# A selective-scan layer inside a two-layer transformer kernel: C's rows in SBUF and the scan's items in pairs

## The chip, the cores and the metric

The kernel is one program on one core of a Trainium2 chip. Its time is the device time of one execution in microseconds (us), as the median of several. In the profile PE is the tensor engine (PEld its weight loads), DVE the vector engine, ACT the scalar engine, POOL GpSimd and SP the engine from whose queue nearly all DMAs are issued.

## The reference

The input is x, 8 rows of 512 time steps and 256 channels. Two layers are added to it, each a conditioned attention part and a conditioned expert part:

```python
x = x + attn0(cond0(x))     # attn0: a selective state-space layer (below)
x = x + ffn0(cond2_0(x))    # 8 experts, top 2, gelu MLP
x = x + attn1(cond1(x))     # 8 heads of softmax attention over 512 steps
x = x + ffn1(cond2_1(x))    # 32 experts, top 4, swiglu, and a shared swiglu
```

cond0 ends in a normalization of its own; cond2_1 is a small adapter with a layer norm behind it. The part that the change is about is attn0, with 512 inner channels and 16 states:

```python
xc, z = split(x @ W_in.T); xc = silu(conv4(xc))
dt, B, C = split(xc @ W_x.T, [64, 80])
delta = softplus(dt @ W_dt.T + b_dt); A = -exp(A_raw)
# over time, for every inner channel d and state n:
h[n, d] = exp(delta[d] * A[n, d]) * h[n, d] + delta[d] * B[n] * xc[d]
y[d] = sum_n C[n] * h[n, d] + D[d] * xc[d]
out = (y * silu(z)) @ W_out.T
```

## The kernel before

Time lies along the free axis (T = 512), channels along the 128 partitions; a row of 256 channels is a tile [128, 2, 512], all in fp32. Two Python generators emit the work. thread_x does attn0 for the eight rows and stores each finished row to DRAM (xa). thread_y does ffn0 and attn1 for groups of rows ([0], [1, 2], [3, 4, 5], [6, 7]). The main loop at the end draws from both in turn by the numbers that they yield (XROW, YROW and others are the totals that it expects), so that group q runs beside the rows of group q + 1. Every engine works through its instructions in the order in which they were emitted, with the two threads mixed; in_order also fixes the order within thread_x on each engine. Behind the last group stand top4's routing and the 32 experts of ffn1.

thread_x itself has two interleaved parts:

- head(b) computes cond0 and everything of attn0 ahead of the scan for row b, in 65 pieces. Its PSUM tiles come from gx(), two banks in turn. It writes delta and delta * xc to DRAM (packs), xc and silu(z) as well (xzs), and keeps bf16 parts of B and C in bc3 (rows[b]). The tile xc (8 KB a partition) also serves soma earlier in the head.
- The scan of row b has 64 items (j, g, k): 4 blocks j of 128 channels, 4 groups g of states, 4 quarters k of 32 channels. One item is 4 states x 32 channels on the 128 partitions. begin(n) emits the decay exp(delta * A) on ACT (L752) and the input delta * xc * B on POOL (L754); run(n) emits the scan on DVE (L780) and the product with C (L781), in place in h. B's rows for a group, spread over the partitions by a matmul, are copied from PSUM to SBUF once per row and group (get_B4, L733). C's rows are spread anew for every j and g, into a PSUM bank of their own (tag c4, in run), from which L781 reads. add(n) sums the states of a finished group by matmuls with fold (L790); gate adds D * xc and multiplies with silu(z); finish projects with W_out, adds x (L809 loads it, L814 adds) and stores the row (L818).

Step n of the loop emits begin(n + 2), run(n), what is due at n, and one piece of the head (two when i % 12 is 4). Without a limit the head moves 69 pieces a row of scan, four more than it has. The PSUM banks are: gx 2, c4 1, yp 1 for thread_x, g 2 and acc 2 for thread_y.

The other places that the diff touches: layernorm (L99 and L100, used by top4's routing), scores in thread_y (the softmax of 128 score rows for two heads at a time: row maximum L1052, exp with the row's sum L1055, reciprocal L1056, scaling L1057), and the shared expert in top4, which takes thread_x's banks yp and c4 for its two sums.

Of the kernel before, what the change touches and what calls it, by code (L numbers as in the profile page):

```python
# [17 lines left out]
P = 128  # L18
# [33 lines left out]
def adaln_attn_ffn_kernel(ctx: ExitStack, tc: tile.TileContext, d: dict, out: bass.AP):  # L52
# [34 lines left out]
    def layernorm(pool, ps_tile, o, bufs=1):  # L87

        mean = ps_tile()
        mm(mean, [(onesdiv, o[:, k, :]) for k in range(KC)])  # L90
        cen = pool.tile([P, KC, T], F32, tag="ln_c", name="ln_c", bufs=bufs)
        nc.vector.tensor_tensor(cen, o, rep(mean, KC), ALU.subtract)
        yield 1
        sq = pool.tile([P, KC, T], F32, tag="ln_q", name="ln_q", bufs=bufs)
        nc.gpsimd.tensor_tensor(sq, cen, cen, ALU.mult)
        var = ps_tile()
        mm(var, [(onesdiv, sq[:, k, :]) for k in range(KC)])
        rstd = pool.tile([P, T], F32, tag="ln_r", name="ln_r", bufs=bufs)
        nc.scalar.activation(rstd, var, AF.Sqrt, bias=epst)  # L99
        nc.vector.reciprocal(rstd, rstd)  # L100
        return cen, rstd
# [294 lines left out]
    def thread_x(wp, wk, ps):  # L396
# [5 lines left out]
        def gx():  # L402
            return ps.tile([P, T], F32, tag="gx", name="gx", bufs=2)
# [18 lines left out]
        W_out = load("W_out", [P, 4, C])  # L422
# [48 lines left out]
        def head(b):  # L471
# [100 lines left out]
            cen = wk.tile([P, KC, T], F32, tag="cen", name="cen")  # L572
# [146 lines left out]
        got, B4s = {}, {}  # L719
# [8 lines left out]
        def get_B4(b, g):  # L728

            pt = gx()  # L730
            mm(pt, [(states(g), rows[b])])
            t = wk.tile([P, T], F32, tag="B4", name="B4", bufs=4)
            nc.scalar.copy(t, pt)  # L733
            B4s[b, g] = t
# [8 lines left out]
        due, product = {}, []  # L743
        items = [(b, j, g, k) for b in range(NB) for j in range(4) for g in range(4) for k in range(4)]
        yps, Cs, hs, dAs, xz, y8s = {}, {}, {}, {}, {}, {}

        def begin(n):
# [3 lines left out]
            dA = wk.tile([P, T], F32, tag="dA", name="dA", bufs=4)  # L751
            nc.scalar.activation(dA, t[:, 0, :], AF.Exp, scale=A[:, 4 * j + k, g : g + 1])  # L752
            h = wk.tile([P, T], F32, tag="h", name="h", bufs=8)
            nc.gpsimd.tensor_tensor(h, t[:, 1, :], B4s[b, g], ALU.mult)  # L754
            hs[n], dAs[n] = h, dA
# [3 lines left out]
            if j == 0 and g < 3 and k == 1:  # L759
                get_B4(b, g + 1)  # L760
# [5 lines left out]
            if j == 3 and b + 1 < NB and g == 3:  # L766
                if k == 0:
                    get_pack(b + 1, 0, 0)
                if k < 3:
                    get_pack(b + 1, 0, k + 1)  # L770
                if k == 3:
                    get_B4(b + 1, 0)

        def run(n):
            b, j, g, k = items[n]
            h = hs[n]
            if k == 0:
                Cs[0] = ps.tile([P, T], F32, tag="c4", name="c4")
                mm(Cs[0], [(states(4 + g), rows[b])])
            nc.vector.tensor_tensor_scan(h, dAs.pop(n), h, 0.0, ALU.mult, ALU.add)  # L780
            product[:] = [nc.vector.tensor_tensor(h, h, Cs[0], ALU.mult).ins]  # L781
            if k == 3:
                due.setdefault(n + 1, []).append(lambda: add(n - 3))

        def add(n):

            b, j, g, _ = items[n]
            if g == 0:
                yps[0] = ps.tile([P, T], F32, tag="yp", name="yp")
            chain([nc.tensor.matmul(  # L790
                yps[0][32 * k : 32 * k + 32, :], fold, hs.pop(n + k), start=(g == 0), stop=(g == 3)) for k in range(4)])
            if g == 3:
                if j == 0:
                    y8s[b] = wk.tile([P, 4, T], F32, tag="y8", name="y8")
                due.setdefault(n + 5, []).append(lambda: gate(b, j, n + 6))
# [8 lines left out]

        def finish(b, e, n, x=None):

            if e == 0:
                x = wk.tile([P, KC, T], F32, tag="cen", name="xr")
                nc.sync.dma_start(x, d["x"][b])  # L809
            pt = gx()  # L810
            mm(pt, [(W_out[:, j, ts(e, P)], y8s[b][:, j, :]) for j in range(4)])
# [11 lines left out]
        def pieces():  # L823

            for b in range(NB):
                for i, _ in enumerate(head(b)):
                    if b == 0 and i == 14:
                        prepare()
                    yield
# [7 lines left out]
        get_B4(0, 0)  # L837
# [3 lines left out]
        for n in range(N):  # L841
            b, i = divmod(n, 64)
            if i == 58 and b + 1 < NB:
                while b + 1 not in ready:
                    next(H)
                    yield 0
            if n + 2 < N:
                begin(n + 2)
            run(n)
            for f in due.pop(n, ()):  # L850
                f()
            next(H, None)
            if i % 12 == 4:
                next(H, None)
            yield 4
        while due:
# [5 lines left out]
    def thread_y(q, bs, ps):  # L862
# [103 lines left out]
        with ExitStack() as ph:  # L966
            wk = ph.enter_context(tc.tile_pool(name=f"k3_{q}", bufs=1))
            H = 8
            for r, b in enumerate(bs):
# [47 lines left out]
                for hp in range(H // 2):  # L1017
# [20 lines left out]
                    def scores(i):  # L1038
# [9 lines left out]
                        read.clear()  # L1048
                        for u in range(2):
# [4 lines left out]
                            den = wk.tile([P, 1], F32, tag="den", name="den", bufs=4)  # L1054
                            read.append(nc.scalar.activation(ex, sp, AF.Exp, bias=nm, accum_out=den).ins)  # L1055
                            nc.vector.reciprocal(den, den)  # L1056
                            nc.scalar.activation(ex, ex, AF.Identity, scale=den)  # L1057
                            exs[i, u] = ex

# [29 lines left out]
    def top4(wp, wk, ps):  # L1089
# [7 lines left out]
        def ps_tile():  # L1097
            return ps.tile([P, T], F32, tag="gx", name="g4", bufs=2)
# [3 lines left out]
        def route(b):  # L1102
# [42 lines left out]
            yp = [ps.tile([P, T], F32, tag=t, name="y4p") for t in ("yp", "c4")]  # L1145
# [215 lines left out]
```

## Time and profile before

| | |
|---|---|
| median of 3 runs | 4148.91 us (4148.35 to 4155.98) |
| the profiled execution | 4169.97 us, span 4168.2 us |
| PE busy | 3258.9 us, 78% of the span |
| DVE busy | 2635.8 us, 63% |
| ACT busy | 1799.2 us, 43% |
| POOL busy | 1612.5 us, 39% |
| rows stored by thread_x at | 442, 781, 1071, 1419, 1743, 2050, 2565, 2882 us |

A line of a group names the kernel's line, the engine, the operation, what it writes and reads (out<-in), the shapes and the count; then come the busy time in us and the mean ns of one, and last the idle time of the engine ahead of these instructions with what ended it. A wait line reads "A <- B: us in total, times, longest". In a table by stage, each engine has its busy us and the number of its instructions, then the granted clock of PE as a share, the DMA engines' busy share and GB/s. A float32 matmul shows as four instructions.

### The profile page before, as it was taken

The numbers are of one execution on the slowest core, as the hardware profiler recorded it, in microseconds if no ns is written. First come the engines' busy times: TensorE is split into PE (matmuls) and PEld (weight loads), VectorE is DVE, ScalarE is ACT, GpSimd is POOL, SyncE is SP. The second block draws the span as 40 slices with busy tenths as digits, with TensorE's granted clock in tenths as the row PEclk, the third lists the DMA queues.
The fourth block names the chain that finished last, engine by engine and source line by source line (L and its number), as shares of the span: only waits on it lengthen the run. The fifth ranks groups of instructions, "written<-read, shape, count | busy, mean of one in ns | idle before, by whom it ended". The sixth has DMA issues, their size and how long they took to land. (4 is left out here: it accounts for less than half of the span.)

```text
span 4168.2 us, 36840 instructions
## 1 busy us (share of the span) xinstructions
PE 3258.9 (78%) x10964; PEld 1653.5 (40%) x10964; DVE 2635.8 (63%) x4178; ACT 1799.2 (43%) x2890; POOL 1612.5 (39%) x1222
## 2 busy tenths in 40 slices
PE   4425586888577788798669698889988999969894
PEld 1101153333254333333337433333466444437772
DVE  4597886798966888888972555764432443433336
ACT  2425465457267367357345333442322343322222
POOL 0445645355536435336353421320043111134552
PEclk7656687998788899799889799999989999989996
DMA  4555676445345312312245312213044112118776
GB/s 107 204 182 205 216 280 217 152 176 206 129 162 163 95 49 84 97 58 74 83 147 187 125 51 72 63 53 100 23 177 146 56 49 75 36 59 260 244 237 223
DMA packets 159372, 554.77 MB, mean 133 GB/s; under 512 B 27731, under 2 KB 34290, under 8 KB 146757
## 3 DMA queue, kind: packets, MB, share of 16 engines
q1 hardware_dynamic: 135076, 501.35, 36.3%
q0 software_dynamic: 24096, 51.08, 3.3%
q8 instruction: 87, 1.43, 0.1%
q14 instruction: 113, 0.92, 0.1%
HBM read 453.00 MB, written 234.82 MB: 165 GB/s over the span
## 5 line engine op out<-in xcount | busy, mean ns | idle before, releaser
L754 POOL TENSOR_TENSOR h<-packed,B 128x512 f32<-128x512 f32 x512 | 813.0, 1610 | 895.4 <-PE yp L790 536.6
L780 DVE TENSOR_TENSOR_SCAN h<-dA,h 128x512 f32<-128x512 f32 x512 | 791.8, 1546 | 77.1 <-POOL h L754 55.6
L752 ACT ACTIVATE dA<-packed,Aexp 128x512 f32<-128x512 f32 x512 | 357.7, 717 | 497.6 <-DVE h L780 346.3
L174 POOL DMA_INDIRECT tok<-ys,to_i x310 | 313.6, 1012 | 456.1 <-DVE ys L959 222.3
L1082 PE MATMUL acc<-aT,V 128*128 128x512 f32 x1024 | 454.3, 598 | 4.1 <-DVE aT L1066 3.9
L781 DVE TENSOR_TENSOR h<-h,c 128x512 f32<-128x512 f32 x512 | 350.1, 684 | 81.5 <-PE c L78 67.5
L174 POOL DMA_INDIRECT tab<-row,si x192 | 198.3, 1033 | 511.3 <-issue 235.4
L1082 PEld LDWEIGHTS acc<-aT,V 128*128 128x128 f32 x1024 | 193.5, 191 | 248.6 <-issue 231.6
L78 PE MATMUL acc<-wv,c 128*128 128x512 f32 x512 | 262.3, 630 | 4.7 <-DVE aT L1066 3.1
L1052 DVE TENSOR_REDUCE nm<-g 128x1 f32<-128x512 f32 x256 | 164.4, 682 | 115.9 <-PE g L1042 114.4
L78 PE MATMUL g<-xT,fw 128*128 128x256 f32 x960 | 231.2, 394 | 7.8 <-ACT h L952 7.8
L78 PE MATMUL acc<-fw,h 128*128 128x256 f32 x960 | 223.1, 386 | 5.2 <-DVE ys L959 5.2
L78 PE MATMUL c<-bc,quads 96*128 96x512 bf16 x128 | 57.8, 451 | 209.0 <-DVE h L781 205.5
L790 PE MATMUL yp<-h,fold 128*32 128x512 f32 x1024 | 217.5, 742 | 0.7 <-DVE h L781 0.7
L1055 ACT ACTIVATE ex<-g,nm 128x512 f32<-128x512 f32 x256 | 173.6, 683 | 102.8 <-DVE nm L1052 98.2
L78 PEld LDWEIGHTS g<-xT,fw 128*128 128x128 f32 x960 | 186.7, 199 | 44.7 <-ACT h L952 9.4
L78 PEld LDWEIGHTS acc<-fw,h 128*128 128x128 f32 x960 | 184.7, 194 | 44.9 <-issue 8.3
L1065 PE MATMUL acc<-ident,ex 128*128 128x128 f32 x1024 | 154.1, 283 | 53.6 <-ACT ex L1057 17.1
L1057 ACT ACTIVATE ex<-ex,den 128x512 f32<-128x512 f32 x256 | 176.6, 720 | 35.3 <-DVE den L1056 34.5
L1086 DVE TENSOR_TENSOR x<-x,acc 128x512 f32<-128x512 f32 x64 | 43.6, 682 | 231.2 <-PE acc L1082 231.2
L1065 PEld LDWEIGHTS acc<-ident,ex 128*128 128x128 f32 x1024 | 118.9, 143 | 176.3 <-issue 51.5
L1042 PE MATMUL g<-qk 64*128 64x512 f32 x512 | 159.8, 671 | 33.2 <-ACT ex L1055 20.6
(284 smaller groups left out, 5720.4 us busy)
## 6 DMA issues: line engine op xcount, KB each, us to landing
fw<-in_fW SPq DMA_DIRECT2D x60, 1154.0 KB
tab<-zeros SPq DMA_DIRECT2D x32, 2112.0 KB
packed<-pack SPq DMA_DIRECT2D x128, 512.0 KB
mw<-in_mW SPq DMA_DIRECT2D x95, 384.0 KB
tab<-zeros SPq DMA_DIRECT2D x16, 2080.0 KB
xt<-tab SPq DMA_DIRECT2D x95, 264.0 KB
pack<-dd SPq DMA_DIRECT2D x32, 512.0 KB
xz<-xzs SPq DMA_DIRECT2D x32, 512.0 KB
```

What stands on the lines that cost most here:

```text
L78: nc.tensor.matmul(o, lhsT, rhs, start=(i == 0), stop=(i == len(pairs) - 1))
L174: i = nc.gpsimd.indirect_dma_start(out=table_, out_offset=bass.IndirectOffsetOnAxis(ap=idx, axis=0), in_=src, in_offset=None, bounds_check ...
L752: nc.scalar.activation(dA, t[:, 0, :], AF.Exp, scale=A[:, 4 * j + k, g : g + 1])
L754: nc.gpsimd.tensor_tensor(h, t[:, 1, :], B4s[b, g], ALU.mult)
L780: nc.vector.tensor_tensor_scan(h, dAs.pop(n), h, 0.0, ALU.mult, ALU.add)
L781: product[:] = [nc.vector.tensor_tensor(h, h, Cs[0], ALU.mult).ins]
L790: chain([nc.tensor.matmul(yps[0][32 * k : 32 * k + 32, :], fold, hs.pop(n + k), start=(g == 0), stop=(g == 3)) for k in range(4)])
L1052: nc.vector.tensor_reduce(nm, sp, AX.X, ALU.max, negate=True)
L1055: read.append(nc.scalar.activation(ex, sp, AF.Exp, bias=nm, accum_out=den).ins)
L1057: nc.scalar.activation(ex, ex, AF.Identity, scale=den)
L1065: nc.tensor.transpose(tp[:, m, :], ex[:, ts(m, P)], ident)
L1082: nc.tensor.matmul(ys[k], V[:, m, C * u + P * k : C * u + P * (k + 1)], aTs[u][:, m, :], start=(u == 0 and m == 0), stop=(u == 1 and m == 3))
```

## The change

- The scan's items are taken in pairs. Two decays lie side by side in one of two fixed tiles, two h tiles likewise. In an even step one scan of 1024 columns runs over both (the second half starts afresh, because the decay's first column there is a zero that is written once); in an odd step one product covers both.
- get_rows replaces get_B4: it spreads and copies C's rows to SBUF beside B's, once per row and group, and the product reads C from there. The bank c4 is gone.
- gx has three banks; top4's shared expert takes one of them in c4's place.
- W_out is no longer loaded once at the start. get_fin loads it and x for each row into a tile that shares xc's buffer, in the fourth step of the next row's scan, one step ahead of finish. The head is held so that it enters row b + 2 by no more than its first piece while row b is scanned. cen shares gm's buffer.
- In scores both row sums lie in one tile, with one reciprocal behind both exps and then both scalings.
- layernorm takes exp(-0.5 ln(var + eps)) on ACT instead of a square root on ACT and a reciprocal on DVE.

```diff
@@ layernorm
-        nc.scalar.activation(rstd, var, AF.Sqrt, bias=epst)
-        nc.vector.reciprocal(rstd, rstd)
+        nc.scalar.activation(rstd, var, AF.Ln, bias=epst)
+        nc.scalar.activation(rstd, rstd, AF.Exp, scale=-0.5)
@@ thread_x
-            return ps.tile([P, T], F32, tag="gx", name="gx", bufs=2)
+            return ps.tile([P, T], F32, tag="gx", name="gx", bufs=3)
...
-        W_out = load("W_out", [P, 4, C])
...
-            cen = wk.tile([P, KC, T], F32, tag="cen", name="cen")
+            cen = wk.tile([P, KC, T], F32, tag="gm", name="cen")
...
-        def get_B4(b, g):
-
-            pt = gx()
-            mm(pt, [(states(g), rows[b])])
-            t = wk.tile([P, T], F32, tag="B4", name="B4", bufs=4)
-            nc.scalar.copy(t, pt)
-            B4s[b, g] = t
+        def get_rows(b, g):
+
+            for t, u in (("B4", g), ("C4", 4 + g)):
+                pt = gx()
+                mm(pt, [(states(u), rows[b])])
+                q = wk.tile([P, T], F32, tag=t, name=t, bufs=4)
+                nc.scalar.copy(q, pt)
+                four[t, b, g] = q
...
+        decays = []
+        for i in range(2):
+            t = wp.tile([P, 2, T], F32, tag=f"dA{i}", name=f"dA{i}")
+            nc.vector.memset(t[:, 1, 0:1], 0.0)
+            decays.append(t)
 
         def begin(n):
 
             b, j, g, k = items[n]
             t = got[b, j, k]
-            dA = wk.tile([P, T], F32, tag="dA", name="dA", bufs=4)
-            nc.scalar.activation(dA, t[:, 0, :], AF.Exp, scale=A[:, 4 * j + k, g : g + 1])
-            h = wk.tile([P, T], F32, tag="h", name="h", bufs=8)
-            nc.gpsimd.tensor_tensor(h, t[:, 1, :], B4s[b, g], ALU.mult)
-            hs[n], dAs[n] = h, dA
+            u = n % 2
+            nc.scalar.activation(decays[n // 2 % 2][:, u, u:], t[:, 0, u:], AF.Exp, scale=A[:, 4 * j + k, g : g + 1])
+            if u == 0:
+                hs[n // 2] = wk.tile([P, 2, T], F32, tag="h", name="h", bufs=4)
+            nc.gpsimd.tensor_tensor(hs[n // 2][:, u, :], t[:, 1, :], four["B4", b, g], ALU.mult)
...
-        def run(n):
-            b, j, g, k = items[n]
-            h = hs[n]
-            if k == 0:
-                Cs[0] = ps.tile([P, T], F32, tag="c4", name="c4")
-                mm(Cs[0], [(states(4 + g), rows[b])])
-            nc.vector.tensor_tensor_scan(h, dAs.pop(n), h, 0.0, ALU.mult, ALU.add)
-            product[:] = [nc.vector.tensor_tensor(h, h, Cs[0], ALU.mult).ins]
-            if k == 3:
-                due.setdefault(n + 1, []).append(lambda: add(n - 3))
+        def scan(m):
+            b, j, g, k = items[2 * m]
+            h, dA = (t.rearrange("p u t -> p (u t)") for t in (hs[m], decays[m % 2]))
+            nc.vector.tensor_tensor_scan(h, dA, h, 0.0, ALU.mult, ALU.add)
+
+        def read(m):
+            b, j, g, k = items[2 * m]
+            nc.vector.tensor_tensor(hs[m], hs[m], rep(four["C4", b, g], 2), ALU.mult)
+            if k == 2:
+                due.setdefault(2 * m + 2, []).append(lambda: add(2 * m - 2))
...
+        fin, at = {}, [0, 0]
+
+        def get_fin(b):
+
+            assert at[0] <= b + 1 or at[1] < 8
+            fin[b] = wk.tile([P, 4, T], F32, tag="xc", name="fin")
+            nc.sync.dma_start(fin[b][:, 0:2, :].rearrange("p k (a c) -> p (k a) c", a=2), d["W_out"])
+            nc.sync.dma_start(fin[b][:, 2:4, :], d["x"][b])
+
         def finish(b, e, n, x=None):
 
             if e == 0:
-                x = wk.tile([P, KC, T], F32, tag="cen", name="xr")
-                nc.sync.dma_start(x, d["x"][b])
+                x = fin[b][:, 2:4, :]
             pt = gx()
-            mm(pt, [(W_out[:, j, ts(e, P)], y8s[b][:, j, :]) for j in range(4)])
+            w = fin[b][:, 0:2, :].rearrange("p k (a c) -> p (k a) c", a=2)
+            mm(pt, [(w[:, j, ts(e, P)], y8s[b][:, j, :]) for j in range(4)])
...
+            if n % 2 == 0:
+                scan(n // 2)
+            else:
+                read(n // 2)
+            if b > 0 and i == 3:
+                get_fin(b - 1)
             if n + 2 < N:
                 begin(n + 2)
-            run(n)
             for f in due.pop(n, ()):
                 f()
-            next(H, None)
-            if i % 12 == 4:
-                next(H, None)
+            for _ in range(1 + (i % 12 == 4)):
+                if at[0] <= b + 1:
+                    next(H, None)
             yield 4
+        get_fin(NB - 1)
@@ thread_y, scores
+                        den = wk.tile([P, 2], F32, tag="den", name="den", bufs=4)
...
-                            den = wk.tile([P, 1], F32, tag="den", name="den", bufs=4)
-                            read.append(nc.scalar.activation(ex, sp, AF.Exp, bias=nm, accum_out=den).ins)
-                            nc.vector.reciprocal(den, den)
-                            nc.scalar.activation(ex, ex, AF.Identity, scale=den)
+                            read.append(nc.scalar.activation(ex, sp, AF.Exp, bias=nm, accum_out=den[:, u : u + 1]).ins)
                             exs[i, u] = ex
+                        nc.vector.reciprocal(den, den)
+                        for u in range(2):
+                            nc.scalar.activation(exs[i, u], exs[i, u], AF.Identity, scale=den[:, u : u + 1])
@@ top4
-            return ps.tile([P, T], F32, tag="gx", name="g4", bufs=2)
+            return ps.tile([P, T], F32, tag="gx", name="g4", bufs=3)
...
-            yp = [ps.tile([P, T], F32, tag=t, name="y4p") for t in ("yp", "c4")]
+            yp = [ps.tile([P, T], F32, tag="yp", name="y4p"), ps_tile()]
```

More of the change, by code (lines that the diff above doesn't have):

```diff
@@ L718, in thread_x @@
         xzs = [dram.tile([P, 4, 2, T], F32, name=f"xzs{i}", tag=f"xzs{i}") for i in range(2)]
-        got, B4s = {}, {}
+        got, four = {}, {}
         def get_pack(b, j, k):
@@ L742, in thread_x @@
         ready = set()
-        due, product = {}, []
+        due = {}
         items = [(b, j, g, k) for b in range(NB) for j in range(4) for g in range(4) for k in range(4)]
-        yps, Cs, hs, dAs, xz, y8s = {}, {}, {}, {}, {}, {}
+        yps, hs, xz, y8s = {}, {}, {}, {}
+        decays = []
[3 more added lines that the diff above has]
+            decays.append(t)
         def begin(n):
@@ L759, in begin @@
             if j == 0 and g < 3 and k == 1:
-                get_B4(b, g + 1)
+                get_rows(b, g + 1)
             if j < 3 and (g, k) == (2, 3):
@@ L771, in begin @@
                 if k == 3:
-                    get_B4(b + 1, 0)
-        def run(n):
-            b, j, g, k = items[n]
-            h = hs[n]
-            if k == 0:
-                Cs[0] = ps.tile([P, T], F32, tag="c4", name="c4")
-                mm(Cs[0], [(states(4 + g), rows[b])])
-            nc.vector.tensor_tensor_scan(h, dAs.pop(n), h, 0.0, ALU.mult, ALU.add)
-            product[:] = [nc.vector.tensor_tensor(h, h, Cs[0], ALU.mult).ins]
-            if k == 3:
-                due.setdefault(n + 1, []).append(lambda: add(n - 3))
+                    get_rows(b + 1, 0)
+        def scan(m):
[7 more added lines that the diff above has]
+                due.setdefault(2 * m + 2, []).append(lambda: add(2 * m - 2))
         def add(n):
@@ L789, in add @@
                 yps[0] = ps.tile([P, T], F32, tag="yp", name="yp")
+            hh = [hs.pop(n // 2), hs.pop(n // 2 + 1)]
             chain([nc.tensor.matmul(
-                yps[0][32 * k : 32 * k + 32, :], fold, hs.pop(n + k), start=(g == 0), stop=(g == 3)) for k in range(4)])
+                yps[0][32 * k : 32 * k + 32, :], fold, hh[k // 2][:, k % 2, :], start=(g == 0), stop=(g == 3))
+                for k in range(4)])
             if g == 3:
@@ L828, in pieces @@
                         prepare()
+                    at[:] = [b, i]
                     yield
@@ L836, in thread_x @@
             get_pack(0, 0, k)
-        get_B4(0, 0)
+        get_rows(0, 0)
         begin(0)
```

## Prediction

> **What bounds the kernel now.** I read the page first, then busy time by stage, then the groups of the scan's loop, then the waits of DVE. All sums are made against the profiled execution: its span is 4168.2 us and its own time 4169.97 us, 0.5% above the median of the three runs (4148.91 us); I take the change in us from the one and put it on the other.
>
> The first cut is by stage. I set the limits at the start of the first scan (154 us), at the first and third of the stores of finished rows (442, then 1071; I put 1100), where rows 0 to 5 are through (2150), at the last row (2882; 2890), and at the end of the attention (3690).
>
> ```profile
> span 4168.2 us, 36840 instructions
> core 0: us, PE busy (x) PEld busy (x) DVE busy (x) ACT busy (x) POOL busy (x), PEclk, DMA share, GB/s
> 0.00:154.00 154.00, 67.82 (x139) 27.22 (x139) 63.64 (x97) 45.10 (x59) 13.59 (x24) 0.76 0.50 149
> 154.00:440.00 286.00, 124.85 (x285) 33.13 (x286) 244.69 (x224) 133.34 (x171) 180.84 (x105) 0.61 0.54 195
> 440.00:1100.00 660.00, 500.19 (x1585) 229.06 (x1588) 544.15 (x700) 361.97 (x521) 325.64 (x216) 0.85 0.57 203
> 1100.00:2150.00 1050.00, 821.20 (x2630) 376.83 (x2623) 875.07 (x1155) 566.87 (x851) 504.72 (x349) 0.87 0.30 95
> 2150.00:2890.00 740.00, 642.68 (x2183) 323.82 (x2182) 389.42 (x589) 302.86 (x547) 217.11 (x155) 0.94 0.30 97
> 2890.00:3690.00 800.00, 741.72 (x2495) 389.89 (x2493) 311.52 (x770) 273.33 (x513) 168.15 (x167) 0.96 0.25 84
> 3690.00:4168.00 478.00, 360.47 (x1658) 273.52 (x1656) 207.32 (x646) 115.74 (x231) 202.43 (x209) 0.87 0.67 216
> ```
>
> From 154 to 2150 us DVE is busy for 1664 of 1996 us (83%) and PE for 1446: there DVE sets the pace. From 2150 on PE does (87%, 93%), and DVE has half its time free. So an edit on DVE is paid before 2150 us, an edit on PE after it.
>
> ```profile
> L754 POOL TENSOR_TENSOR h<-packed,B 128x512 f32<-128x512 f32 x512 | 813.0, 1610 | 895.4 <-PE yp L790 536.6
> L780 DVE TENSOR_TENSOR_SCAN h<-dA,h 128x512 f32<-128x512 f32 x512 | 791.8, 1546 | 77.1 <-POOL h L754 55.6
> L781 DVE TENSOR_TENSOR h<-h,c 128x512 f32<-128x512 f32 x512 | 350.1, 684 | 81.5 <-PE c L78 67.5
> L78 PE MATMUL c<-bc,quads 96*128 96x512 bf16 x128 | 57.8, 451 | 209.0 <-DVE h L781 205.5
> ...
> L780 DVE TENSOR_TENSOR_SCAN h<-dA,h x512: 1184/1219/6939, 154.9 to 2830.2; 128x512 f32<-128x512 f32 x171
> L781 DVE TENSOR_TENSOR h<-h,c x512: 656/686/690, 156.3 to 2831.4; 128x512 f32<-128x512 f32 x171
> L590 DVE TENSOR_TENSOR cen<-cen,rstd x8: 1218/1222/1228, 98.7 to 2119.1; 128x1024 f32<-128x1024 f32 x8
> ```
>
> In the second half of this fence the three numbers are the least, the median and the longest ns. Scan and product are 1142 us of DVE. The scan's mean (1546) is far above its median (1219), with a tail to 6939; the product never leaves 656 to 690. Sorted by whether a GpSimd tensor operation runs beside them, 275 scans take 1832 ns in the mean and 237 take 1215; products take 684 in both cases. The scan reads two SBUF tensors, the product one and C from PSUM.
>
> ```profile
> DVE h L781 <- PE c L78: 55.2, 17, 11.9
> DVE to_m L331 <- DMA xt<-tab: 45.3, 8, 11.7
> DVE h L780 <- POOL h L754: 42.9, 9, 20.3
> L588 ACT ACT_TABLE_LOAD x8: 1283/1283/1283, 96.7 to 2116.6; - x8
> L100 DVE RECIPROCAL ln_r<-ln_r x8: 3343/3353/3356, 3017.5 to 3704.4; 128x512 f32<-128x512 f32 x8
> ```
>
> The first three lines are DVE's longest waits from 154 to 2150 us (us, times, longest): the product behind C's matmul leads. The last two serve the small edits below.
>
> **The change part by part.**
>
> Pairs. 684 ns at 512 columns and 1222 at 1024 give 538 per 512 and 146 ns fixed. A scan of 1024 columns has no row; as a lone scan is 1215, the pair is estimated at 1215 + 1069 = 2284 instead of 2430, the paired product at 1222 (L590's row, same form, both inputs in SBUF) instead of 1368. That is 0.29 us a pair; 35, 67 and 104 pairs lie in the three DVE-bound stages (71, 134, 207 scans): 60 us, with another 15 after 2150 us that PE covers (worth nothing there; if PE were not in front, 15 more). The reset by a zero column costs nothing: exp writes 511 columns instead of 512. The depth is kept: two pairs of decays for four single ones, four pairs of h for eight, and the group's add stands at the same step, so POOL waits for PE's yp as before.
>
> C from SBUF. Here a rule speaks against the change. Row first: the scan above, 1215 alone and 1832 beside GpSimd, the product 684 always. The rule is the Trainium skill's, page "SBUF — State Buffer", section "Who interferes with whom": a DVE instruction with two SBUF inputs contends with a GpSimd instruction that reads SBUF, and the lock is exclusive, for the whole instruction. The timeline from 1504.8 to 1511.3 us agrees: scan and L754 alternate at 2.16 us an item, 1.08 each, and the product hides beside L754. With C in SBUF the product joins this queue. By the rule at its hardest, each product meets a whole GpSimd operation, 1.08 us. By the trace, the rest of a GpSimd tensor operation that runs when a product starts is 0.60 us in the mean over all products from 154 to 440 us and 0.33 and 0.30 in the next two stages. A pair had two scans that waited 0.34 us each (1546 less 1215, a little less); it will have one scan and one product. If the scan waits as it did and the product as just said, the pair pays about what it paid; but a scan no longer has an open product ahead of it beside which GpSimd may run, so I take 0.12 us a pair more (bounds 0, and 0.75 with every product blocked whole). Net -0.17 us x 206 pairs = -35 us.
>
> C's matmuls. 128 become 32: 96 x 0.45 = 43 us of PE, of which about 19 matmuls, 8 us, lie from 2150 to 2890 us, where PE sets the end. PE's wait ahead of them (205.5 us) does not go: in the same step the yp matmuls (L790) wait for the same product, so it moves to yp. DVE's wait for C (67.5 us, 55.2 of it where DVE is the bound) goes, since C4 is copied a group ahead; next in DVE's order come operations that wait for the same late PE (gm, the other thread's L331 and L1086), so I count half: -28 us (bounds 0 and -60). ACT gets 32 copies more at 579 ns (the row of the B copy), 19 us; ACT is busy half the time, and the copy stands right behind B's, for which ACT waits anyway: nothing, at most +10 if exp is held up.
>
> W_out and x per row. SP issues both loads one step ahead of PE's first use; ahead of the issue stands only the wait for xc's last reader on POOL (L668). The old load of x (L809) was issued 17 to 147 us before its row was stored, so SP runs ahead of PE; behind it in SP's queue stand the packed loads, four steps from their use. If they land late, PE stops at the projection with the other thread's matmuls behind it: between 0 and 8 us a row (lora, 320 KB, held the chain for 6.2 us). I take 1 us a row: +8. Sharing xc with soma of the row after next delays nothing, ten steps lie between; cen in gm's buffer likewise.
>
> The head's cap. It ran four pieces a row further ahead; at 2150 us it had some 17 pieces of row 7 done, about 20 us of DVE (a gated round is 1.22 + 2 x (1.37 + 0.92) = 5.8 us). They now fall after 2150 us, where DVE is free; their matmuls, about 8 us, go to the PE-bound stage: -14 + 8 = -6.
>
> Third bank. Of 27 us that PE waited for gm's two rows in the first 154 us much is data, not banks: -3 (bounds 0 and -15).
>
> den. 128 reciprocals of 154 ns go, 20 us; rows 0 to 2 run before 2150 us: -7. The first scaling waits for both exps, 0.25 us for ACT, hidden: from 2900 to 3000 us PE is busy for 100.00 of 100.
>
> Layer norm. Eight reciprocals of 3.35 us for an Exp of 0.63; seven are covered by PE. The Trainium skill (page "ScalarE: Activation LUTs", section "Table sets") puts ln and exp into one set, with one table load; here L588 loads again before Exp, 1.28 us, every time, and the trace decides: 3.35 - 1.91 = 1.4 us for the last row, and the softmax's Exp behind it saves its load: -3 (by the page -4).
>
> Sum: -35 - 28 + 8 (loads) - 6 - 8 (PE) - 3 - 7 - 3 = -82. 4149 - 82 = 4067 us.
>
> **The rivals.** (a) The port takes it all. Every paired product stands behind a whole L754, +0.75 us a pair: 0.63 more than taken, x 206 = +130, so 4197 us. For it: POOL bursts four h in a row when a group is added, just as two scans and two products are due, and in the first scans 60% of the products start with GpSimd busy. Against: after 440 us it is a third, and between scan and product lie the head's and the other thread's operations, and those of them that read PSUM, as the product did, leave GpSimd its turn. From +0.52 us a pair on the change is slower. (b) The waits only move: DVE's wait for PE returns whole behind gm and the scans' wait for POOL, and the port eats the 0.29. What is left is -7 - 6 - 8 - 3 - 3 + 8 = -19: 4130 us. For it: PE is at 76 to 78% from 440 to 2150 us, so DVE can't run far ahead. (c) The two threads come apart: both idle shares (DVE 291 us, PE 389 us from 440 to 2150) shrink, by another 80 us: 3987.
>
> **How the numbers follow.** My forecast 0.55, (a) 0.19, (b) 0.19, (c) 0.07. The forecast's own range is 4015 to 4125. The range of 3975 to 4197 reaches to (a) and (c) and leaves out a stronger port loss, and any gain beyond both. About 0.2% is what a measurement of this kernel can tell from no change (8 us). Faster: the forecast, (c) and most of (b): 0.76. Same 0.06, the rest of (b) and the edge of the forecast. Slower 0.18, nearly all of (a).
>
> **What would show it.** Right: 256 scans of 1024 columns, median near 2.28 us, mean 2.6 to 2.8; 256 products with least near 1.22 and now a tail, mean near 1.6; no DVE wait for C; PE's wait for DVE at L790 where it was at C; DVE's busy time before the sixth row's store down by some 40 us, that store 60 us or more earlier. Wrong: a product's mean above 2.0 us (the port, a), PE waiting for W_out's load in a row's fourth step, or scans waiting for POOL's h where they did not. The forecast fails if the stage before 2150 us is not shorter, whatever PE does after it.

## The result: slower by 3.2%

The changed kernel takes 4283.62 us in the median of 4 runs (4273.67 to 4289.23), against 4151.03 (4148.35 to 4155.98) for the kernel before on the same chip: ratio 1.0315, 95% interval 1.0293 to 1.0338, some 132 us slower. The forecast was 82 us faster, and its range ended at 4197.

The first fence is the table by stage of the changed kernel, cut at the store of the sixth row and at the point where thread_y has stored rows 3 to 5; the second is the kernel before with the same two marks. The columns are those of the table in the prediction.

```profile
span 4280.7 us, 35900 instructions
155.00:2099.00 1944.00, 1408.36 (x4199) 611.55 (x4200) 1555.10 (x1420) 1023.79 (x1507) 1070.75 (x615) 0.83 0.42 145
2099.00:3125.00 1026.00, 860.08 (x2790) 420.92 (x2789) 557.53 (x748) 396.01 (x715) 318.99 (x208) 0.90 0.27 87
```

```profile
154.00:2050.00 1896.00, 1385.36 (x4297) 611.38 (x4297) 1568.70 (x1887) 1024.07 (x1488) 951.98 (x620) 0.83 0.43 148
2050.00:3009.00 959.00, 822.55 (x2749) 406.08 (x2749) 529.18 (x867) 383.47 (x691) 278.22 (x204) 0.92 0.28 92
```

The loss comes in two halves: 48 us until the sixth row is stored (1944 against 1896), where DVE was to be relieved, and 67 us in the next stage (1026 against 959), where PE sets the pace. From there to the end both take about the same (1156 and 1159 us). (The two profiled executions lie 112 us apart; that of the kernel before was some 20 us above its median.) In the first stage DVE has 14 us less to do and is idle for 62 us more; POOL is busy for 119 us more. In the second, PE is idle for 166 us instead of 136 and busy for 38 more, at a granted clock of 0.90 instead of 0.92.

The scan's groups of the changed kernel, then the least, median and longest ns of scan and product, then the longest waits of DVE and of PE from 155 to 2099 us:

```profile
L762 POOL TENSOR_TENSOR h<-packed,B 128x512 f32<-128x512 f32 x512 | 899.4, 1779 | 740.6 <-PE yp L798 453.5 <-DMA packed<-pack 191.7 <-ACT dA L759 26.9
L784 DVE TENSOR_TENSOR_SCAN h<-dA,h 128x1024 f32<-128x1024 f32 x256 | 696.4, 2720 | 215.3 <-POOL h L762 122.3 <-ACT dA L759 85.7 <-PE g L1016 4.4
L788 DVE TENSOR_TENSOR h<-h,C 128x1024 f32<-128x1024 f32 x256 | 399.6, 1561 | 2.6
L784 DVE TENSOR_TENSOR_SCAN h<-dA,h x256: 2253/2292/8906, 155.9 to 2868.4; 128x1024 f32<-128x1024 f32 x128
L788 DVE TENSOR_TENSOR h<-h,C x256: 1185/1224/3335, 158.2 to 2871.2; 128x1024 f32<-128x1024 f32 x128
...
DVE h L784 <- POOL h L762: 94.0, 22, 24.9
DVE h L784 <- ACT dA L759: 70.3, 26, 8.1
...
PE yp L798 <- DVE h L788: 198.0, 39, 13.0
```

Scan and product together fall from 1142 to 1096 us, about what the forecast had (0.17 us for each of 256 pairs is 44 us), and DVE's wait for C (67.5 us) is gone. But the scan, which waited for 77 us in all, now waits for 215, for POOL's h and ACT's decay, and POOL's own operations are longer: 1779 ns for h where it was 1610. PE's wait has moved to yp.

### The profile page after: what moved, and what is told of

Its sections match the earlier page's. It is cut to its first block, busy times and chain, and to the rows that moved or that the text cites. A ratio compares the mean times of both kernels' runs of the same rounds, so it can differ in the third digit from the quotient of the medians.

```text
span 4280.7 us, 35900 instructions
## 1 busy us (share of the span) xinstructions
PE 3298.8 (77%) x10868; PEld 1662.1 (39%) x10868; DVE 2615.9 (61%) x3524; ACT 1817.3 (42%) x2940; POOL 1774.0 (41%) x1222
## 5 line engine op out<-in xcount | busy, mean ns | idle before, releaser
L762 POOL TENSOR_TENSOR h<-packed,B 128x512 f32<-128x512 f32 x512 | 899.4, 1779 | 740.6 <-PE yp L798 453.5
L784 DVE TENSOR_TENSOR_SCAN h<-dA,h 128x1024 f32<-128x1024 f32 x256 | 696.4, 2720 | 215.3 <-POOL h L762 122.3
L759 ACT ACTIVATE dA<-packed,Aexp 128x512 f32<-128x512 f32 (+1 forms) x512 | 351.4, 716 | 526.3 <-DVE h L784 350.1
L174 POOL DMA_INDIRECT tok<-ys,to_i x310 | 338.3, 1091 | 481.6 <-DVE ys L984 227.0
L798 PE MATMUL yp<-h,fold 128*32 128x512 f32 x1024 | 287.8, 731 | 308.4 <-DVE h L788 218.7
L788 DVE TENSOR_TENSOR h<-h,C 128x1024 f32<-128x1024 f32 x256 | 399.6, 1561 | 2.6
L174 POOL DMA_INDIRECT tab<-row,si x192 | 213.0, 1110 | 451.3 <-issue 115.6
L331 DVE SCALAR_TENSOR_TENSOR to_m<-xt,sc_teb 128x8 f32<-128x8 f32 (+1 forms) x155 | 50.8, 327 | 284.8 <-DMA xt<-tab 284.8
L798 PEld LDWEIGHTS yp<-h,fold 128*32 128x32 f32 x1024 | 37.0, 117 | 462.6 <-issue 434.2
L541 DVE TENSOR_TENSOR_SCAN tr<-alpha,gm 128x512 f32<-128x512 f32 x128 | 191.4, 1495 | 3.8 <-POOL y L809 3.5
```

Source lines behind the costliest of these rows:

```text
L174: i = nc.gpsimd.indirect_dma_start(out=table_, out_offset=bass.IndirectOffsetOnAxis(ap=idx, axis=0), in_=src, in_offset=None, bounds_check ...
L541: nc.vector.tensor_tensor_scan(tr, alpha[:, 1 + i : 2 + i].to_broadcast([P, T]), gm[:, k, :], 0.0, ALU.mult, ALU.add)
L759: nc.scalar.activation(decays[n // 2 % 2][:, u, u:], t[:, 0, u:], AF.Exp, scale=A[:, 4 * j + k, g : g + 1])
L762: nc.gpsimd.tensor_tensor(hs[n // 2][:, u, :], t[:, 1, :], four["B4", b, g], ALU.mult)
L784: nc.vector.tensor_tensor_scan(h, dA, h, 0.0, ALU.mult, ALU.add)
L788: nc.vector.tensor_tensor(hs[m], hs[m], rep(four["C4", b, g], 2), ALU.mult)
```

## Experiments: which part costs

At first three theories stood: a pair's second item is emitted only one step ahead of its scan (look-ahead); the compiled order lets thread_x run further ahead of thread_y on PE (order); the product from SBUF meets GpSimd (port). Ratios are to the kernel before, run on the same chip. Where two kernels ran on different chips, they are compared by these ratios.

**Single items, C from SBUF (e1).** In each step one scan and one product of 512 columns:

```diff
+        def one(n):
...
             nc.vector.tensor_tensor_scan(h, dA, h, 0.0, ALU.mult, ALU.add)
...
+            nc.vector.tensor_tensor(h, h, four["C4", b, g], ALU.mult)
...
-            if n % 2 == 0:
-                scan(n // 2)
-            else:
-                read(n // 2)
+            one(n)
```

> The changed kernel with the items taken singly again: one scan of 512 columns and one product with C from SBUF per step; all else stays as changed. Three theories for the 132 us lost. Look-ahead (L): a scan of a pair needs the decay and the input of its second item, which were emitted only one step ahead of it, where every item had two steps; single items get that back, so the waits of the scan for ACT's decay and POOL's h fall from 208 us toward the 77 us of before, and the time to about 4190. Order on PE (O): the compiled order of PE puts 2600 instead of 2715 of the other thread's matmuls ahead of the scans' last group, and the missing ones are done at the end; here it is 2668, so about 40% of the loss is left in the end part: about 4215 to 4245. Port (P): the product from SBUF stands behind GpSimd; single items keep that and pay 0.29 us a pair more: 4300 or above.

Measured: 4277.6 us, 1.0328 (1.0292 to 1.0364): no better than the pairs, though the scan's waits are those of before.

```profile
L784 DVE TENSOR_TENSOR_SCAN h<-dA,h 128x512 f32<-128x512 f32 x512 | 820.0, 1602 | 73.8 <-POOL h L762 56.6 <-ACT dA L759 16.9
L785 DVE TENSOR_TENSOR h<-h,C 128x512 f32<-128x512 f32 x512 | 504.5, 985 | 11.9
L785 DVE TENSOR_TENSOR h<-h,C x512: 664/692/2696, 153.0 to 2909.8; 128x512 f32<-128x512 f32 x171
```

The product takes 985 ns in the mean where it took 684. Sorted by whether a GpSimd tensor operation runs beside it, 298 products take 690 ns and 214 take 1397; before, it was 684 in both cases. DVE has 154 us of products more to do.

**The pairs alone, on the kernel before (e2).** C stays in PSUM:

```diff
+            if n % 2 == 0:
+                h, dA = (t.rearrange("p u t -> p (u t)") for t in (hs[m], decays[m % 2]))
+                nc.vector.tensor_tensor_scan(h, dA, h, 0.0, ALU.mult, ALU.add)
+            else:
+                nc.vector.tensor_tensor(hs[m], hs[m], rep(Cs[0], 2), ALU.mult)
```

> The kernel before with the pairs alone: two decays in one of two fixed tiles, one scan of 1024 columns, one product of 1024 columns with C read from its PSUM bank as before. L: the pair's scan waits as in the changed kernel, so most of the loss is here, 4220 to 4260. O: 2672 of the other thread's matmuls stand ahead of the last scan group (2715 before, 2600 changed), so +20 to +45: 4170 to 4195. P: the product reads PSUM and does not meet GpSimd, and the pairs' fixed cost is saved: 4090 to 4130.

Measured: 4193.85 us, 1.0116 (1.0077 to 1.0155). DVE's busy time falls from 2635.8 to 2554.2 us, and the kernel is slower. Order's range held that, at its edge; the port expected a gain, the look-ahead a larger loss.

**The 2 by 2.** Two more kernels close the square: the changed kernel with C back in the bank c4 (gx with two banks), with single items (e5) and with pairs (e6).

```diff
-            for t, u in (("B4", g), ("C4", 4 + g)):
+            for t, u in (("B4", g),):
...
+            if k == 0:
+                Cs[0] = ps.tile([P, T], F32, tag="c4", name="c4")
+                mm(Cs[0], [(states(4 + g), rows[b])])
```

> The changed kernel without its two main parts: single items, and C spread by matmul into the bank c4 for every block and group and read from there, as before (so gx has two banks again). What stays are the loads of W_out and x per row, the head's limit, the decays in two fixed tiles, den and the layer norm. Set beside the kernel with single items and C from SBUF (4278 us), it differs in C's source alone. Port (P): the product goes back from 985 to 684 ns, 154 us of DVE's busy time, of which about 110 lie where DVE sets the pace: 4140 to 4170, as the kernel before. Loads (a rival: what stays costs the time, W_out and x come late or the head's limit starves PE): 4230 to 4280. Order on PE: 2727 matmuls of the other thread stand ahead of the last scan group, as many as before (2715): 4140.

> The changed kernel with only C put back: pairs, but C spread by matmul into the bank c4 and read from PSUM by the paired product (gx two banks). P: the product falls from 1561 to about 1215 ns, 88 us of DVE, and the time to that of the pairs alone, 4185 to 4205; C from SBUF then costs a pair 80 to 100 us and two single items about 130. Loads: 4250 to 4284. If pairs were harmless and only C's place cost: 4140 or less. The pairs alone gave 4194.

| | C from PSUM | C from SBUF |
|---|---|---|
| single items | 4142.09 us, 0.9992 (0.9983 to 1.0002) | 4277.6 us, 1.0328 (1.0292 to 1.0364) |
| pairs | 4202.62 us, 1.0144 (1.0127 to 1.0161) | 4283.62 us, 1.0315 (1.0293 to 1.0338) |

What stays in e5 (the loads per row, the head's limit, den, layer norm) costs nothing. By the ratios, C from SBUF costs 3.4% (about 139 us) with single items and 1.7% (about 71 us) with pairs. Pairs cost 1.5% (60 us, on one chip) with C in PSUM, and nothing that can be told from noise with C in SBUF. The third bank of gx comes and goes with C's place; no run separates the two. The stage until the sixth row's store, of e5, of e6 and of e1, in this order:

```profile
154.00:2024.00 1870.00, 1378.24 (x4271) 603.38 (x4272) 1522.82 (x1805) 1024.13 (x1490) 947.33 (x616) 0.84 0.43 151
157.00:2028.00 1871.00, 1364.13 (x4272) 603.88 (x4273) 1458.33 (x1414) 1014.30 (x1488) 952.54 (x616) 0.83 0.43 151
151.00:2108.00 1957.00, 1479.55 (x4200) 618.82 (x4201) 1673.84 (x1819) 1032.08 (x1506) 941.96 (x617) 0.83 0.41 144
```

Pairs take 64 us from DVE's busy time and nothing from the stage. C from SBUF adds 151 us to DVE's busy time and 87 to the stage with single items; with pairs (e6 to the changed kernel) it adds 97 us to DVE, 118 to POOL and 73 to the stage. Each row is one execution: before and e5, whose medians agree, differ by 26 us in this stage (1896 and 1870), so differences of that size say little. But in none of the other kernels with pairs and C in PSUM (e2 above, and those that follow) is the stage shorter than in e5: it takes 1876 to 1921 us. Over the whole run scan and product show where the pairs' saving went, first in e5, then in e6:

```profile
L787 DVE TENSOR_TENSOR_SCAN h<-dA,h 128x512 f32<-128x512 f32 x512 | 789.8, 1543 | 74.8 <-POOL h L762 59.7 <-ACT dA L759 13.3 <-POOL dd L665 1.6
L788 DVE TENSOR_TENSOR h<-h,c 128x512 f32<-128x512 f32 x512 | 349.7, 683 | 51.2 <-PE c L78 36.8 <-DVE h L787 0.5
```

```profile
L762 POOL TENSOR_TENSOR h<-packed,B 128x512 f32<-128x512 f32 x512 | 806.2, 1598 | 862.2 <-PE yp L801 549.3 <-DMA packed<-pack 194.9 <-ACT B L733 39.7
L787 DVE TENSOR_TENSOR_SCAN h<-dA,h 128x1024 f32<-128x1024 f32 x256 | 683.8, 2671 | 230.0 <-POOL h L762 133.5 <-ACT dA L759 93.0 <-POOL dd L665 1.7
L791 DVE TENSOR_TENSOR h<-h,c 128x1024 f32<-128x1024 f32 x256 | 310.0, 1211 | 22.6 <-PE c L78 18.7 <-DVE h L787 0.5
```

The pairs save 146 us of busy time here (1139.5 less 993.8). The scan's idle time grows by 155 us and the product's falls by 29, so 126 of them come back as waits.

## Experiments: is it look-ahead or order?

**Look-ahead (e3, e9, e8).** e3: the changed kernel with begin three steps ahead. e9: pairs, C in PSUM, three steps ahead and three tiles of decays. e8: pairs, C in PSUM, scan and product both in the odd step.

```diff
-            if n + 2 < N:
-                begin(n + 2)
+            if n + 3 < N:
+                begin(n + 3)
```

```diff
-            if n % 2 == 0:
+            if n % 2 == 1:
                 scan(n // 2)
-            else:
                 read(n // 2)
```

> The changed kernel with each item's decay and input emitted three steps ahead of its own step instead of two, so that the second item of a pair has two steps before the scan as every item had before; still two decay tiles. L: the scan's wait for ACT and POOL falls by half or more, 4170 to 4220. O: 2588 of the other thread's matmuls stand ahead of the last scan group (2600 in the changed kernel), so no gain: 4280 to 4300. P: no change, 4284. Against L: the third step puts the first decay of the next pair right behind the scan that frees its tile, so part of the wait may stay.

> Pairs with C in PSUM, begin three steps ahead and three tiles of decays instead of two, so that ACT need not wait for the last scan. Look-ahead: 4120 to 4160, with the waits of the scan for ACT near 15 us. Grain: 4190 to 4215. Order on PE: 2668 matmuls as in the pairs, so 4203.

> Pairs with C in PSUM (4203 us), but scan and product of a pair both in its odd step, so the second item's decay and input again have two steps before the scan; no buffer more. C's source and the rest are as in the kernel with single items (4142 us), so the 60 us between the two are the pairs' own. Look-ahead: the scan's waits for ACT and POOL (93 and 134 us in the pairs, 13 and 60 singly) fall to the single ones and the time to 4120 to 4160. Grain (a scan of 2.3 to 3 us holds up DVE's other work, and with it ACT, PE and the other thread): no gain, 4190 to 4215. Order on PE: 2715 matmuls of the other thread ahead of the last scan group (2668 in the pairs, 2727 singly): 4150.

Measured: e3 4286.58 us, 1.0358 (1.0315 to 1.0401); e9 4223.35, 1.0217 (1.0197 to 1.0237); e8 4196.62, 1.0141 (1.0124 to 1.0158). No gain from any. The scan's wait falls from 215 to 128 us in e3 and from 230 to 140 in e9; most of what goes is the wait for ACT, and most of that for POOL's h stays. The groups of e8:

```profile
L787 DVE TENSOR_TENSOR_SCAN h<-dA,h 128x1024 f32<-128x1024 f32 x256 | 669.4, 2615 | 81.3 <-POOL h L762 61.4 <-ACT dA L759 19.4
L791 DVE TENSOR_TENSOR h<-h,c 128x1024 f32<-128x1024 f32 x256 | 311.3, 1216 | 102.0 <-PE c L78 95.1 <-DVE h L787 0.5
```

The scan's wait falls from 230 to 81 us, as the theory has it, and the time stays: 80 of these 149 us come back in the product's wait (23 to 102), nearly all of it for C's matmul. Look-ahead falls as the cause of the time, though it is the cause of that wait.

**Order on PE (e4, e7).** Each piece of thread_x's PE work is held behind the PE work that thread_y had emitted just before (e4) or 265 instructions earlier (e7, shown; e4 takes the last one):

```diff
+            ahead = front[-265] if len(front) >= 265 else None
             for i in nc.cur_bb.bb.instructions[n:]:
+                if ahead is not None and i.engine == mybir.EngineType.PE:
+                    tc.add_manual_dep(i, ahead.name, NOSYNC)
+                    ahead = None
```

> The changed kernel with one more constraint on the compiled order: each piece of thread_x's PE work stands behind the PE work that thread_y had emitted before it. 2980 instead of 2600 matmuls of thread_y then stand ahead of the scans' last group. O: the end part behind the last row's store shrinks by the 115 missing matmuls and more, 4284 less 65 to 100: 4185 to 4220. L: the scans wait as much or more, and nothing is won: 4270 to 4300, or slower if PE holds thread_x up behind thread_y's waits. P: no change, 4284.

> The changed kernel, with thread_x's PE work held behind what thread_y had emitted 265 PE instructions earlier: 2727 matmuls of thread_y then stand ahead of the scans' last group (2600 in the changed kernel, 2715 before), and the order up to the seventh row stays that of the changed kernel. Order (O): the end part shrinks by the missing matmuls and the last row is stored little later: 4215 to 4245. P, or any cause on DVE: the last row is stored later by what the end part gains, 4275 to 4300. The full constraint (2980 matmuls) gave 4352.

Measured: e4 4352.11 us, 1.0507 (1.0472 to 1.0543); e7 4272.12, 1.0303 (1.0286 to 1.0321). In e7 the part behind the last row's store falls from 1350 to 1167 us and that store comes 174 us later: what the end wins, the scans lose. Order falls as well, for the changed kernel, in which it was tried.

**Which half of the pair (e10, e11).** C in PSUM; e10 (first diff) pairs only the scan, e11 (second diff) only the product.

```diff
+            for u in range(2):
+                nc.vector.tensor_tensor(hs[m][:, u, :], hs[m][:, u, :], Cs[0], ALU.mult)
```

```diff
-            if n % 2 == 0:
-                scan(n // 2)
-            else:
+            scan(n // 2, n % 2)
+            if n % 2 == 1:
                 read(n // 2)
```

> Pairs with C in PSUM, only the scan paired: in the odd step two products of 512 columns instead of one of 1024. It costs 146 ns a pair more DVE. Look-ahead and grain: the paired scan is the cause, so 4195 to 4215. If the paired product were the cause (h is given to PE later): 4140 to 4160.

> Pairs with C in PSUM, only the product paired: a scan of 512 columns in each step, one product of 1024 columns in the odd step. Look-ahead and grain: 4135 to 4150, the kernel with single items or a little under it (the paired product saves 146 ns of fixed cost, some 25 us before the sixth row is stored). If the paired product were the cause: 4195 to 4210.

Measured: e10 4205.79 us, 1.0168 (1.0151 to 1.0185); e11 4196.19, 1.0135 (1.0116 to 1.0155). Either half alone costs what the pair costs. So the long scan is not needed for the loss, and it is not only the wait for the second item: in e11 the scan waits 107 us, half of the pairs' 230.

**The mix of the threads (e12, e13, e14, e17).** Only the constant XROW, with which the main loop weighs thread_x against thread_y, is changed from 256: 272 and 248 in the kernel before, 248 and 272 with pairs and C in PSUM.

```diff
-XROW, YROW, YGROUP, YTILE, P4ROW = 256.0, 242.0, 20.0, 9.0, 10.0
+XROW, YROW, YGROUP, YTILE, P4ROW = 272.0, 242.0, 20.0, 9.0, 10.0
```

> The kernel before with one constant of the main loop changed: XROW, the total that a row of thread_x is expected to yield, 272 instead of 256, so that thread_x is drawn further ahead of thread_y. No operation changes. 2672 matmuls of thread_y stand ahead of the scans' last group (2715 before; 2668 and 2672 in the kernels with pairs and C in PSUM). Mix (the pairs cost only because they shift how the two threads are mixed, so that thread_x is through early and thread_y's attention stands alone on PE): 4170 to 4210, as the pairs. Rival, the pairs' own cost on DVE: the mix is not sharp, 4130 to 4160.

> The kernel before with XROW 248: thread_x is drawn a little later, 2727 matmuls of thread_y ahead of the last group (2715). Mix: 4125 to 4160, near the optimum for which 256 stands. Rival: the same. If it is faster by over 10 us, the constants of before are no optimum.

> Pairs with C in PSUM (4203 us) with XROW 248: 2715 matmuls of thread_y ahead of the last group instead of 2668, 2272 instead of 2252 ahead of the seventh row's. Mix: 4140 to 4170, most of the 60 us comes back. Rival, the pairs' own cost: 4190 to 4215.

> Pairs with C in PSUM with XROW 272. The kernel before did not change from 256 to 272 (4139 against 4134) and lost 34 us at 248; the pairs lost 36 us at 248. Mix (the pairs have their optimum at a larger constant): 4150 to 4185. Rival, the pairs' own cost: 4195 to 4220.

Measured: before with 272 4139.49 us, 1.001 (0.9996 to 1.0024), with 248 4168.65, 1.0092 (1.0059 to 1.0124); pairs with 248 4239.52, 1.0269 (1.0242 to 1.0296), with 272 4247.28, 1.0224 (1.0191 to 1.0257). No operation changes, and the time moves by up to 1.2%. The pairs are best at 256 of the three values, so neither of the other two would have saved them.

**Twelve h buffers (e15, e16, e18).** In the room that C's copies leave, h gets six tiles of two items instead of four; single items, pairs, and pairs with the late scan of e8 (all with C in PSUM).

```diff
-                hs[n // 2] = wk.tile([P, 2, T], F32, tag="h", name="h", bufs=4)
+                hs[n // 2] = wk.tile([P, 2, T], F32, tag="h", name="h", bufs=6)
```

> The kernel with single items and C in PSUM (4142 us), with 12 h buffers instead of 8 (six tiles of two items instead of four), in the room that the resident W_out and x leave. No operation changes. Ring (POOL waits 592 us for the matmuls that free h, DVE waits 60 us for POOL's h: PE, POOL and DVE go round eight buffers): the wait of the scan for POOL falls, and the sixth row is stored 20 to 60 us earlier: 4080 to 4125. Rival (the waits are where the engines meet PE's two threads, and more buffers only move them): 4130 to 4155.

> Pairs with C in PSUM (4203 us), with six tiles of h of two items instead of four. Ring: a pair's first scan needs two inputs from POOL, so it feels the eight buffers more than single items do (134 against 60 us of waiting); with twelve the waits fall, and the time to 4110 to 4150. Rival: 4185 to 4215.

> Pairs with C in PSUM, twelve h buffers, and scan and product of a pair both in its odd step: both changes that eased a wait of the pairs, together. Twelve buffers gave back 0.8% of the pairs' 1.4%, the late scan nothing by itself though the scan's wait fell from 230 to 81 us. If what is left of the pairs' loss is the scan's wait for POOL and ACT: 4100 to 4150. Rival (the pairs' grain: what DVE saves is turned into waits elsewhere, and the other thread waits longer for DVE and ACT): 4165 to 4200.

Measured: single items 4156.7 us, 1.0002 (0.9986 to 1.0019); pairs 4181.58, 1.0060 (1.0039 to 1.0081); pairs with the late scan 4219.3, 1.0142 (1.0116 to 1.0168). The groups of POOL's h and of the scan in e16:

```profile
L762 POOL TENSOR_TENSOR h<-packed,B 128x512 f32<-128x512 f32 x512 | 833.2, 1651 | 612.7 <-DMA packed<-pack 359.6 <-PE yp L801 122.1 <-ACT B L733 111.8
L787 DVE TENSOR_TENSOR_SCAN h<-dA,h 128x1024 f32<-128x1024 f32 x256 | 675.4, 2638 | 210.0 <-POOL h L762 110.9 <-ACT dA L759 97.4 <-issue 1.2
```

POOL's wait for the matmuls that free h falls from 549 to 122 us. With single items (592 to 162 us) that buys nothing, with pairs 0.8 of the 1.4%. So more than half of the pairs' loss goes with four more buffers. But the scan's own wait falls only from 230 to 210 us, with the late scan the gain is gone, and 0.8% is no more than a mere change of the mix has moved: by which way the buffers help is not settled.

No version beat the kernel before; e5, e12 and e15 equal it.

## Why the prediction was wrong

**The sum on DVE was right.** From before to after, scan and product go from 4.46 to 4.28 us a pair: -0.18, where -0.17 was forecast. The port's term in it holds too. The 0.12 us were meant as what a pair waits for GpSimd more than the two scans of before. Without such meetings a pair took 3.80 us before (twice 1215 and 684 ns) and takes 3.50 now (2281 and 1215); what is left is 0.66 and 0.78 us. In the changed kernel 136 of the 256 products run beside a GpSimd operation (1866 ns against 1215), which is 0.35 us in the mean over all; the trace's rest of a running GpSimd operation, weighted by the pairs of the three stages, had been 0.36. The rule that the prediction weighed (the Trainium skill, "SBUF — State Buffer", "Who interferes with whom") pointed the right way; its hardest form, a whole GpSimd operation for each product, was too much.

**The failed step: DVE's net was taken as the kernel's change.** A saving (the pairs) and a cost (C's place) on the same engine were set against each other, as if a microsecond of DVE before the sixth row were a microsecond of time either way. The 2 by 2 shows them apart. The saving alone, e5 to e6, takes 64 us off DVE's busy time in that stage, and the stage is 1 us longer: at 81 to 83% busy DVE already waited for what POOL, ACT and PE hand it, and what it saves becomes more of that waiting. The cost alone is paid: +97 us of DVE with pairs make the stage 73 us longer (e6 to the changed kernel), +151 with single items 87 (e5 to e1). Why the one is lost and the other is not is argued from these waits, not shown by a run of its own.

**Terms that were put at nothing.** GpSimd's side of a meeting: with pairs L762 grows from 1598 to 1779 ns when C moves to SBUF, and POOL, for which the scan waits, is 118 us busier before the sixth row. The stage in which PE sets the pace: it was given -8 us for C's matmuls and +8 for the head's, and became 67 us longer, more than half of the loss (below).

**DVE's busy time before the sixth row** was to fall by some 40 us and fell by 14. Scan and product did give 44 us there. But durations of neighbouring instructions overlap in the profile: in this stage before, 1676 us of durations lie in 1569 us of busy time. With fewer instructions there is less of it: 82 us instead of 107, and 82 instead of 100 from e5 to e6, where the pairs alone differ. So some 20 us of what the pairs seem to save had never been time; the 146 ns fixed, taken from durations, count them.

**The rivals.** (a) has, with 4197 us, the nearest number, by luck: it let scan and product grow by 0.46 us a pair, and its mark, a product above 2.0 us, did not come. The change is slower at 0.12 us more a pair, not from 0.52 on. (b), that the waits only move, is what the pairs show, but it let the time stay where it was. (c) had both idle shares shrink; until the sixth row DVE's grew by 62 us and PE's by 25. Of the signs of being wrong two came: the stage before the sixth row's store is not shorter, and scans wait for POOL's h (55.6 to 122.3 us).

**"The depth is kept."** In buffers it is; in waits it isn't. The scan's idle time rose from 77 to 215 us. But e3, e8 and e9, which lower this wait and gain no time, show that it is not by itself the price.

**DVE's wait for C, -28 us.** The wait went (67.5 to 2.6 us), and 138 us of the scan's waits came. PE's wait for DVE moved to yp as forecast (205.5 to 218.7 us).

**The small terms.** Loads, limit, den and layer norm were put at -8 us in sum; e5 holds just these and is 0.9992 (0.9983 to 1.0002) of before, about -3 us. PE waited 12.5 us in all for W_out, 8 having been put down. In the layer norm each of the two operations loads its table, as the trace of before had it for L588 and not as the page cited has it.

```profile
L99 ACT ACT_TABLE_LOAD x8 | 10.3, 1283 | 0.1
L100 ACT ACT_TABLE_LOAD x8 | 10.3, 1283 | 0.1
```

**The PE-bound stage** is 969 us in e5 and 959 before, but 1019 with pairs, 1021 with C in SBUF and 1026 with both. The rows of e5 and e6 and, for each, PE's wait for the tile hi, then the two stages of e8:

```profile
2024.00:2993.00 969.00, 822.32 (x2773) 407.30 (x2772) 553.45 (x842) 391.24 (x702) 288.66 (x207) 0.92 0.28 92
PE acc L1031 <- ACT hi L1028: 4.7, 4, 2.9
2028.00:3047.00 1019.00, 847.81 (x2814) 416.70 (x2813) 532.26 (x743) 397.00 (x715) 300.51 (x208) 0.90 0.27 88
PE acc L1037 <- ACT hi L1034: 21.3, 7, 6.7
159.00:2069.00 1910.00, 1452.45 (x4285) 621.88 (x4285) 1446.91 (x1416) 1026.08 (x1495) 972.87 (x619) 0.85 0.42 148
2069.00:3056.00 987.00, 843.84 (x2763) 410.73 (x2764) 525.28 (x717) 388.34 (x703) 294.24 (x204) 0.91 0.28 90
```

Of the 50 us between e5 and e6, 24 are idle time of PE, and 25 are busy time: 41 more matmul records (12 us at 0.30 us each; nearly all are top4's routing, which e5 does behind this mark) and a lower granted clock. Why PE idles more there is open. A wait that grows in all three (21 us each, 5 in e5 and before) is that of thread_y's matmuls for hi (the hidden tile of cond1) on ACT, whose queue also holds the exps that wait for DVE's scan. In e8, whose scan waits least, it is 5 us again and the stage 987 us. So this path may hold for a part; but in e8 the stage before is longer (1910 us against 1871; its profiled execution was 15 us above its median), so the pairs' loss does not seem tied to one stage.

**What is settled:** moving C to SBUF costs 1.7% (pairs) to 3.4% (single items), and with it the product is 29% to 44% longer; pairs cost 1.5% with C in PSUM, and nothing more once C is in SBUF; the rest costs nothing. Open is how the pairs lose their 60 us: e8 speaks against look-ahead, e11 against the long scan, e14 and e17 against the constant, and order on PE gained nothing in the changed kernel; more than half of it goes with four more h buffers. Open too is how either part reaches the PE-bound stage.

## What to carry to other kernels

Before an operand is moved from PSUM to SBUF, count who else reads SBUF beside that instruction: a copy that saves 43 us of matmuls made the reader 29% (pairs) to 44% (single items) longer. Where one engine is 83% busy and three others hand it buffers, don't set a saving against a cost on that engine: here the saving came back as waits and the cost was paid. Time taken from an engine there is a gain only when the next engine's wait shrinks with it. And where the order of two threads is part of the tuning, 1% is what a mere change of the mix can move, so an edit worth less in busy time may end on either side.

## What the runs showed of the hardware

The granted clock of PE goes with its busy share from stage to stage: 0.62 in a stage where PE is busy for 43% of the time, 0.86 at 77%, 0.89 at 81%, 0.92 at 85%, 0.97 at 94% (the stages of e5; only its last, 0.88 at 76%, is a little out of line). The Trainium skill ("TensorE: Matmul & The Clock Gate", "What's actually happening") says that a gate sets the clock by how busy PE has been just before; the order of these stages agrees. By that a wait of PE would be paid twice, as idle time and in the matmuls behind it: from e5 to e6 the busy share of the PE-bound stage goes from 85% to 83% and its clock from 0.92 to 0.90. No run changed the one alone.

The price of sharing SBUF with GpSimd went by meetings, not by columns. A product with both inputs in SBUF pays 707 ns beside GpSimd at 512 columns (690 to 1397, e1) and 651 at 1024 (1215 to 1866, changed kernel), about the same for twice the work; with C in PSUM it pays nothing (683 ns in both cases in e5, 1210 and 1212 in e6). A paired scan pays 390 ns in the mean (2281 to 2671) where two single scans pay 656 (1215 to 1543, twice): 149 of 256 paired scans met a GpSimd operation (e6), against 275 of 512 single ones (e5), and each meeting costs about the same (672 and 610 ns).
